# Two cross-attention layers in one program: the filler products of the first seven steps dealt out anew

## The chip, the cores and the metric

One Trainium2 chip; the program runs on one of its cores. The metric is the device time of one execution in microseconds (us), the median of several runs. The profile comes from one further look at the same program: the hardware profiler's record of one execution.

## What is computed

Two cross-attention layers follow each other, for 8 batches of 256 queries of width 320 (20 heads of 16) and 256 context tokens of width 512. The context's text tokens and its last few tokens (image tokens) have keys and values of their own.

```python
# layer 0: two softmaxes, 77 text tokens and 179 others
q = heads(x @ Wq.T); k = heads(text @ Wk.T); v = heads(text @ Wv.T)
k_ip = heads(ip @ Wk_ip.T); v_ip = heads(ip @ Wv_ip.T)
x = (attend(q, k, v) + attend(q, k_ip, v_ip)) @ Wo.T + bo + x
# layer 1: 252 text tokens, 4 image tokens
probs_t = softmax(q @ k_t.T * scale)
text_out = probs_t @ v_t
qsem = l2norm(probs_t @ text)              # 512 wide, per head
sem = qsem @ l2norm(ip).T
probs_ip = softmax(q @ k_ip.T * scale + 0.5 * sem) * mask
x = (text_out + probs_ip @ v_ip) @ W_out + b_out + x
```

The norm of `qsem` is taken without `qsem` itself: its square is a quadratic form of the probabilities with the gram matrix of the text tokens (252 x 252).

## The kernel before

The work is cut into steps. Each batch has 5 groups of 4 heads (`NQ` = 5), and step n does group n % 5 of batch n // 5 of layer 0, and, from step 6 on (`SHIFT` = 6), the group n - 6 of layer 1. The change concerns steps 0 to 6; step 7 is the last one with a list of its own. TensorE (PE), VectorE (DVE), ScalarE (ACT) and GpSimd (POOL) each run their instructions in the order in which the program issues them; no scheduler reorders them.

A step, function `both_layers`, issues in this order:

- the scores of the four heads (`scores`, L359), from `sc_qz`, queries with the other heads' rows masked out, and `k0`. The masked queries of step n + 1 (`masked_q`, L349) are made on GpSimd near the end of step n, behind everything that GpSimd was given before;
- the maxima on VectorE (L500), then the exponentials of heads 0 and 1 on ScalarE (L512);
- the fillers of place 0;
- the exponentials of heads 2 and 3;
- the transposes of heads 0 and 1 (L397), each copied to `et` (L404) by VectorE;
- the transposes of the previous group's output, its scaling (L555) and its sum on GpSimd (`attn`, L565);
- the fillers of place 1;
- the transposes of heads 2 and 3, the copy of the last one by ScalarE;
- the fillers of place 2; then the masked queries for the next step; then (from step 6) layer 1's scores, exponentials and transposes with the places 3 to 6;
- the value products of layer 0 (`l0_values`, L530) and the copy `oT_sb` by ScalarE (L540).

A filler is a piece of other work that is put into such a place: a product on TensorE into one of two PSUM buffers (`mm_tile`) and its copy out, the eviction. Its instructions stand in every engine's queue at the place where the filler is issued. The lists of `fillers` are written out by hand. The fillers that the change moves:

- `l0_q(b, ms)`: queries of layer 0, thirds `ms` (L292), evicted by ScalarE (L299). The last third serves group 4.
- `l0_k(b, m)`: keys (L310); for m = 2 four evictions by ScalarE (L468, L472), else one (L462).
- `l0_v(b, i)`: values (L322), evicted by ScalarE (L485, L487). Values have two buffers, one for each of two batches.
- `l1_gram(b, c)`: gram matrix (L621). For c = 0 it is 126 x 252, evicted by ScalarE in three pieces (L630), for c = 1 126 x 126 in one; then GpSimd copies it to nine further places of the tile `gv` (L634). The first layer-1 values that read `gv` are in step 7.
- `ip_squares`, `ip_norm`: squares and norms of all image tokens, on VectorE and ScalarE (a square root, L250, which needs another table of functions than the exponential); `ip_T` transposes them (L259), `ip_k` and `ip_v` make layer 1's image keys (L272) and values.
- `l1_q`, `l1_k`: queries and keys of layer 1.

In step 5 the fillers of place 2 are a chain: `l0_attn_T`, `l0_out`, then `l1_xT` and `l1_q` give layer 1 its first queries. The inputs of the second batch are loaded from ScalarE's queue: `encT` at the start of step 1, `xT` at the start of step 2.

Of the kernel before, what the change touches and what calls it, by code (L numbers as in the profile page):

```python
# [50 lines left out]
def kernel(  # L51
# [40 lines left out]
    def mm_tile(name):  # L92
        return ps_mm.tile([P, 512], F32, tag="mm", name=name)

    def bc(ap, shape):
        return ap.to_broadcast(shape)
# [512 lines left out]
    def l1_gram(b, c):  # L609
        r = bat[b]  # L610
        encT_b = r["encT"]
        if c == 0:
            r["gv"] = [
                bp.tile([TC1, NPAIR, w + 2 * WV], F32, tag=f"gv{i}", name=f"gv{i}_{b}")
                for i, w in enumerate((3 * TC1, TC1))
            ]
        gv = r["gv"][c]
        ps = mm_tile(f"g{c}_{b}")
        n = TXT1 - c * TC1
        for k in range(NE):  # L620
            nc.tensor.matmul(  # L621
                ps[:TC1, :n],
                encT_b[:, k, c * TC1 : (c + 1) * TC1],
                encT_b[:, k, c * TC1 : TXT1],
                start=(k == 0),
                stop=(k == NE - 1),
            )
        blocks = ((TC1, 2.0), (0, 1.0), (TC1, 2.0)) if c == 0 else ((0, 1.0),)
        for i, (t0, f) in enumerate(blocks):
            nc.scalar.mul(  # L630
                gv[:, 0, WV + i * TC1 : WV + (i + 1) * TC1], ps[:TC1, t0 : t0 + TC1], f
            )
        n = len(blocks) * TC1
        nc.gpsimd.tensor_copy(  # L634
            gv[:, 1:, WV : WV + n],
            bc(gv[:, 0, WV : WV + n].unsqueeze(1), [TC1, NPAIR - 1, n]),
        )
# [362 lines left out]
    def fillers(n, place):  # L1000
        b, s = divmod(n, NQ)
        ahead, now, last, old = b + 1, b, b - 1, b - 2
        plan = {
            (0, 0): [(l0_v, now, 2)],
            (0, 1): [(l0_q, now, (2,))],
            (0, 2): [(l0_attn_T, last, 0), (l1_image, old)],
            (0, 3): [(l0_attn_T, last, 1), (l0_out, last, 0), (l0_out, last, 1)],
            (0, 4): [(l1_k, last, 0)],
            (0, 5): [(l1_xT, last)],
            (0, 6): [(l1_q, last, (0, 1))],  # L1010
            (1, 0): [(l0_k, now, 1)],
            (1, 1): [(l1_q, last, (2,))],
            (1, 4): [(l1_k, last, 1)],
            (1, 5): [(l1_ip, now), (l1_gram, now, 0)],
            (2, 0): [(l1_v, now, 0)],
            (2, 1): [(l1_gram, now, 1), (l1_den, old), (l1_norm, old)],
            (2, 2): [(l0_k, now, 2)],
            (2, 4): [(l0_v, ahead, 0), (l1_fused, old)],
            (2, 6): [(l1_fused_exp, old)],
            (3, 0): [(l1_v, now, 1)],  # L1020
            (3, 3): [(l1_probs, old)],
            (3, 4): [(l0_q, ahead, (0, 1))],
            (3, 5): [(l1_probs_T, old), (l1_text, old), (l0_v, ahead, 1)],
            (4, 0): [(l0_k, ahead, 0)],
            (4, 1): [(l1_attn, old)],
            (4, 2): [(l1_attn_T, old, 0)],
            (4, 3): [(l1_attn_T, old, 1)],
            (4, 4): [(l1_out, old, 0)],
            (4, 5): [(l1_out, old, 1)],
        }  # L1030
        if n <= NQ + 2:
            plan = (
                {
                    0: [(l0_v, 0, 0), (l0_v, 0, 1)],
                    1: [(l0_v, 0, 2)],
                },
                {
                    0: [(l0_k, 0, 1)],
                    1: [(l0_k, 0, 2)],
                    2: [(l0_q, 0, (2,))],  # L1040
                },
                {
                    0: [(l1_gram, 0, 0), (l0_v, 1, 0)],
                    1: [(l0_k, 1, 0), (ip_squares, 0)],
                    2: [(ip_norm, 0)],
                },
                {
                    0: [(l0_v, 1, 1), (l0_q, 1, (0, 1))],
                    1: [(ip_T, 0), (l0_v, 1, 2)],
                    2: [(ip_v, 0)],  # L1050
                },
                {
                    0: [(l1_ip, 0), (l1_v, 0, 0), (l1_v, 0, 1)],
                    1: [(ip_k, 0), (l1_gram, 0, 1)],
                    2: [(ip_k, 1)],
                },
                {
                    0: [(l0_k, 1, 1), (ip_k, 2), (l0_q, 1, (2,))],
                    1: [(l1_k, 0, 0)],
                    2: [(l0_attn_T, 0, 0), (l0_attn_T, 0, 1), (l0_out, 0, 0), (l0_out, 0, 1)],  # L1060
                    5: [(l1_xT, 0)],
                    6: [(l1_q, 0, (0, 1))],
                },
                {
                    0: [(l1_k, 0, 1)],
                    1: [(l1_q, 0, (2,))],
                    2: [(l0_k, 1, 2)],
                    4: [(l1_ip, 1), (l1_gram, 1, 0)],
                    5: [(l1_gram, 1, 1)],
                },  # L1070
                {
                    0: [(l1_v, 1, 0)],
                    4: [(l0_v, 2, 0)],
                },
            )[n]
            plan = {(s, at): f for at, f in plan.items()}
        if b >= 3 and b % 2:

            plan[1, 0], plan[1, 1] = plan[1, 0] + plan[1, 1], []
        if b >= 2 and b % 2 == 0 and ahead < B:  # L1080
            plan[3, 4] = [(l0_v, ahead, 1)]
            plan[3, 5] = [(l1_probs_T, old), (l1_text, old), (l0_q, ahead, (0,))]
            plan[4, 0] = [(l0_q, ahead, (1,)), (l0_k, ahead, 0)]
        if (b, s) == (1, 4):
            plan[4, 4] = [(l0_v, ahead, 2)]
        if (b, s) == (2, 0):
            plan[0, 0], plan[0, 1] = plan[0, 1], []
        if b == B - 1:

            plan[0, 6] = []  # L1090
            plan[1, 0] = [(l1_q, last, (0, 1))]
            plan[1, 1] = [(l1_q, last, (2,))]
            plan[1, 5] = [(l0_k, now, 1)]
            plan[2, 0] = [(l1_ip, now), (l1_gram, now, 0)]
            plan[3, 4] = [(l1_k, now, 0)]
            plan[4, 0] = [(l1_v, now, 0)]
        if b == B:
            plan[0, 4] = [(l1_k, last, 1)]
            plan[1, 4] = []
        for f, at, *args in plan.get((s, place), ()):  # L1100
            if 0 <= at < B:
                f(at, *args)
# [22 lines left out]
    def both_layers(n, u, v1):  # L1125
# [7 lines left out]
        if late:  # L1133
            l0_exp(u0, 1)
        fillers(n, 0)
        if not late:
            l0_exp(u0, 1)
# [3 lines left out]
        l0_transposed(u0, 1)  # L1141
        part(l0_attn, u)
        fillers(n, 1)
        part(l1_values, v1, 1, (0,))
        l0_transposed(u0, 2)
        part(l1_values, v1, 1, (1,))

        l0_transposed(u0, 3, nc.vector.tensor_copy if n % NQ == 2 and n > 2 * NQ else None)
        fillers(n, 2)
        part(l1_values, v1, 2)  # L1150
        qz[1] = queries(1, n)
# [125 lines left out]
```

## Time and profile before

| | |
|---|---|
| median of 3 runs | 883.96 us (883.80 to 883.97) |
| the profiled execution | 883.8 us, of it 882.1 us span |
| TensorE busy | 865.1 us, 98% of the span |
| VectorE, ScalarE, GpSimd busy | 614.0, 546.0, 208.8 us |
| granted TensorE clock | 1.00 in all windows of the first 64 us |
| starts of layer 0's scores, steps 0 to 7 | 11.03, 22.50, 33.66, 44.90, 59.70, 71.38, 91.52, 110.32 us |

PE is TensorE's products, PEld its weight loads, which run beside the products before them. In a timeline line stand the start and the length in us, the engine, the line of the source, the operation, the tile written and those read, the shapes and the number of merged instructions, and in brackets the idle time of that engine before it and what ended it. "issue" means that nothing that the profile shows was waited for.

### The profile page before, as it was taken

How to read it: one execution, taken by the hardware profiler on the slowest of the kernel's cores; microseconds unless marked ns; L12 is line 12 of the kernel's file. 1: busy time of each engine (PE TensorE's matmuls, PEld its weight loads, DVE VectorE, ACT ScalarE, POOL GpSimd, SP SyncE). 2: the span in 40 equal slices, each digit the busy share in tenths (PEclk: the TensorE clock that was granted, in tenths of full speed). 3: DMA queues.
4: the chain of work that ended last, by engine and by line, in shares of the span. 5: the costliest groups of instructions: out<-in, count | busy, mean ns of one | idle time of the engine just before them, and what ended most of it. 6: DMA issues, size and time to landing. Idle time of an engine off the chain costs nothing.

```text
span 882.1 us, 18743 instructions
## 1 busy us (share of the span) xinstructions
PE 865.1 (98%) x6178; PEld 696.4 (79%) x6178; DVE 614.0 (70%) x2071; ACT 546.0 (62%) x2386; POOL 208.8 (24%) x376
## 2 busy tenths in 40 slices
PE   9999899999999999999999999999999999999997
PEld 6767678788787887888878888888888787777776
DVE  2544477767777777776778678776777778775765
ACT  4765666656755586555765468654675558654844
POOL 2212311223221222122321322212232122312111
PEclk9999999999999999999999999999999999999999
DMA  9600100001000100011001010000100100000000
GB/s 278 173 6 6 52 2 1 2 16 43 15 2 20 34 25 2 10 27 42 16 1 21 16 43 1 3 20 16 43 1 1 22 16 1 1 21 1 1 20 16
DMA packets 24624, 22.96 MB, mean 26 GB/s; under 512 B 5936, under 2 KB 24496, under 8 KB 24528
## 3 DMA queue, kind: packets, MB, share of 16 engines
q1 hardware_dynamic: 23088, 20.27, 8.7%
q10 hardware_dynamic: 1440, 1.49, 0.5%
q8 instruction: 50, 0.82, 0.4%
q14 instruction: 46, 0.38, 0.1%
HBM read 18.31 MB, written 2.62 MB: 24 GB/s over the span
## 4 chain that ended last, share of the span: by engine, by line
PE 85%; ACT 3%; DVE 1%; issue 0%; POOL 0%; ACTq 0%; DVEq 0%
PE y L752 17%; PE sc L397 15%; PE sc L359 9%; PE y L755 9%; PE v L322 9%; PE k L310 7%; PE q L292 6%; PE p_o L335 5%; PE oT L530 4%; PE g L621 2%; ACT e L728 1%; ACT e L512 1%; PE p_aT_ps L328 1%; PE o L550 1%; PE ipo L866 1%; PE x1T_ps L328 1%
## 5 line engine op out<-in xcount | busy, mean ns | idle before, releaser
L512 ACT ACTIVATE e<-sc,nmx 128x77 f32<-128x77 f32 (+1 forms) x640 | 227.2, 411 | 58.1 <-DVE nmx L500 56.4
L728 ACT ACTIVATE e<-sc,nmx 128x252 f32<-128x252 f32 x320 | 147.4, 484 | 119.5 <-DVE aip L708 106.2
L752 PE MATMUL y<-gv,et 126*128 126x272 f32 x640 | 202.1, 397 | 1.2
L759 DVE CUSTOM_DVE_ANT_0 e<-y,e 128x252 f32<-128x252 f32 x320 | 134.0, 419 | 93.2 <-PE y L755 84.9
L397 PE MATMUL sc<-ident,e 128*126 128x128 f32 (+1 forms) x1280 | 183.2, 274 | 6.2 <-ACT e L512 3.7
L404 DVE COPY et<-sc 128x512 f32<-128x512 f32 (+1 forms) x228 | 153.9, 689 | 24.7 <-PE sc L397 15.5
L500 DVE TENSOR_REDUCE nmx<-sc 128x2 f32<-128x154 f32 x320 | 109.7, 415 | 85.4 <-PE sc L359 85.4
L397 PEld LDWEIGHTS sc<-ident,e 128*126 128x126 f32 (+1 forms) x1280 | 148.7, 140 | 17.6 <-ACT e L512 8.2
L512 ACT ACTIVATION_READ_ACCUMULATOR e<-sc,nmx 128x1 f32 x640 | 159.5, 250 | 0.0
L755 PEld LDWEIGHTS y<-gv,et 126*128 126x128 f32 x640 | 120.7, 189 | 25.9
L755 PE MATMUL y<-gv,et 126*128 126x146 f32 x640 | 131.4, 287 | 0.0
L713 DVE TENSOR_REDUCE nmx<-sc 128x2 f32<-128x504 f32 x160 | 106.7, 674 | 24.2 <-PE sc L359 24.2
L565 POOL TENSOR_TENSOR attn<-o_sb 128x64 f32<-128x64 f32 x80 | 24.4, 327 | 405.4 <-DVE o_sb L555 365.5
L752 PEld LDWEIGHTS y<-gv,et 126*128 126x128 f32 x640 | 104.8, 190 | 18.1 <-issue 3.0
L404 ACT COPY et<-sc 126x512 f32<-126x512 f32 (+1 forms) x92 | 52.9, 593 | 74.2 <-PE sc L397 74.1
L359 PE MATMUL sc<-k,sc_qz 32*128 32x256 f32 x1152 | 82.5, 400 | 1.0 <-POOL sc_qz L349 1.0
L349 POOL TENSOR_SCALAR sc_qz<-q,quad_m 128x256 f32<-128x256 f32 x80 | 73.2, 925 | 7.3 <-ACT q L299 6.7
L359 PEld LDWEIGHTS sc<-k,sc_qz 32*128 32x128 f32 x1152 | 52.0, 184 | 24.4 <-issue 14.8
L728 ACT ACTIVATION_READ_ACCUMULATOR e<-sc,nmx 128x1 f32 x320 | 69.8, 218 | 0.0
L322 PE MATMUL v<-wv,encT 128*126 128x324 f32 (+1 forms) x192 | 58.1, 447 | 0.0
L763 DVE COPY num<-y 128x20 f32<-128x20 f32 x320 | 55.8, 174 | 0.0
L335 PE MATMUL p_o<-wo,p_aT 128*128 128x320 f32 x180 | 53.0, 437 | 0.3 <-DVE p_aT L329 0.3
(151 smaller groups left out, 1047.1 us busy)
## 6 DMA issues: line engine op xcount, KB each, us to landing
encT<-in_encT_dram SPq DMA_DIRECT2D x7, 512.0 KB
x<-in_x_dram SPq DMA_DIRECT2D x8, 320.0 KB
out_dram<-osb SPq DMA_DIRECT2D x15, 160.0 KB
xT<-in_xT_dram SPq DMA_DIRECT2D x7, 256.0 KB
texts<-in_encT_dram SPq DMA_DIRECT2D x6, 154.0 KB
xT<-in_xT_dram SPq DMA_DIRECT2D x7, 128.0 KB
vip_rows<-vipA SPq DMA_DIRECT2D x32, 25.0 KB
wv<-in_WvT_dram SPq DMA_DIRECT2D x1, 640.0 KB
```

Source lines behind the costliest of these rows:

```text
L322: nc.tensor.matmul(ps, lhsT(k), w[:, k, :], start=(k == 0), stop=(k == NE - 1))
L335: nc.tensor.matmul(ps[:, :C], aT[:, m, :], w[:, m, :], start=(m == 0), stop=(m == NC - 1))
L359: nc.tensor.matmul(sc[j][:, half, :], qz[rows, half * P : (half + 1) * P], kT(j)[rows, :], start=True, stop=True,)
L397: nc.tensor.transpose(v[:, c, half, :], u["e"][x][:, i, half, t0 + c * tn : t0 + (c + 1) * tn], ident,)
L404: copy(u["et"][x][:tn, i].rearrange("p c n s -> p (c n s)"), ps)
L500: nc.vector.tensor_reduce(u["nmx"][x][:, j, :, a], u["sc"][2 * x + j][:, :, t0:t1], AX.X, ALU.max, negate=True,)
L512: nc.scalar.activation(u["e"][x][:, j, half, t0:t1], u["sc"][2 * x + j][:, half, t0:t1], AF.Exp, bias=u["nmx"][x][:, j, half, a : a + 1], ...
L713: nc.vector.tensor_reduce(u["nmx"][x][:, j, :], u["sc"][2 * x + j][:, :, t0 : t0 + TXT1], AX.X, ALU.max, negate=True,)
L728: nc.scalar.activation(u["e"][x][:, j, half, t0 : t0 + TXT1], u["sc"][2 * x + j][:, half, t0 : t0 + TXT1], AF.Exp, bias=u["nmx"][x][:, j, ...
L752: nc.tensor.matmul(y, et[:, 1 - odd, half, :], gv[0][:, g, full], start=True, stop=False)
L755: nc.tensor.matmul(y[:, into], et[:, odd, half, :], gv[1][:, g, part], start=False, stop=True)
L759: nc.vector.tensor_tensor_reduce(e, y[:, g0 : g0 + TXT1], e, op0=ALU.mult, op1=ALU.add, scale=1.0, scalar=0.0, accum_out=r["n2"][:, half, ...
```

## The change

The lists for steps 1 to 6 are written anew. Nothing is added or left out. On GpSimd the copy L634 of the small gram part moves from step 4 to step 1, behind that step's `attn` and ahead of the masked queries for step 2; that of the large part stays in step 2 but moves from ahead of `attn` to behind it, again ahead of the masked queries. On ScalarE the evictions move with their products; on VectorE the copies of `ip_T` and `ip_k`. SyncE's queue keeps its order. The first lines let the tile `gv` be made by whichever gram part is issued first.

```diff
--- before.py
+++ after.py
@@ -609,7 +609,7 @@
     def l1_gram(b, c):
         r = bat[b]
         encT_b = r["encT"]
-        if c == 0:
+        if "gv" not in r:
             r["gv"] = [
                 bp.tile([TC1, NPAIR, w + 2 * WV], F32, tag=f"gv{i}", name=f"gv{i}_{b}")
                 for i, w in enumerate((3 * TC1, TC1))
@@ -1035,36 +1035,35 @@
                     1: [(l0_v, 0, 2)],
                 },
                 {
-                    0: [(l0_k, 0, 1)],
+                    0: [(l0_k, 0, 1), (l0_q, 0, (2,))],
                     1: [(l0_k, 0, 2)],
-                    2: [(l0_q, 0, (2,))],
+                    2: [(l1_gram, 0, 1)],
                 },
                 {
-                    0: [(l1_gram, 0, 0), (l0_v, 1, 0)],
+                    0: [(l0_v, 1, 0), (l0_v, 1, 1)],
                     1: [(l0_k, 1, 0), (ip_squares, 0)],
-                    2: [(ip_norm, 0)],
+                    2: [(ip_norm, 0), (l1_gram, 0, 0)],
                 },
                 {
-                    0: [(l0_v, 1, 1), (l0_q, 1, (0, 1))],
-                    1: [(ip_T, 0), (l0_v, 1, 2)],
+                    0: [(l0_q, 1, (0, 1)), (ip_T, 0)],
+                    1: [(l0_v, 1, 2)],
                     2: [(ip_v, 0)],
                 },
                 {
                     0: [(l1_ip, 0), (l1_v, 0, 0), (l1_v, 0, 1)],
-                    1: [(ip_k, 0), (l1_gram, 0, 1)],
-                    2: [(ip_k, 1)],
+                    1: [(ip_k, 0), (ip_k, 1)],
+                    2: [(ip_k, 2)],
                 },
                 {
-                    0: [(l0_k, 1, 1), (ip_k, 2), (l0_q, 1, (2,))],
+                    0: [(l0_k, 1, 1), (l0_q, 1, (2,))],
                     1: [(l1_k, 0, 0)],
                     2: [(l0_attn_T, 0, 0), (l0_attn_T, 0, 1), (l0_out, 0, 0), (l0_out, 0, 1)],
                     5: [(l1_xT, 0)],
                     6: [(l1_q, 0, (0, 1))],
                 },
                 {
-                    0: [(l1_k, 0, 1)],
-                    1: [(l1_q, 0, (2,))],
-                    2: [(l0_k, 1, 2)],
+                    0: [(l1_k, 0, 1), (l1_q, 0, (2,))],
+                    1: [(l0_k, 1, 2)],
                     4: [(l1_ip, 1), (l1_gram, 1, 0)],
                     5: [(l1_gram, 1, 1)],
                 },
```

## The prediction

> **What bounds the kernel now.** I read the page first, then the timeline of the first 112 us one engine at a time: TensorE's weight loads, ScalarE, GpSimd, VectorE. The page's first part and its chain say that TensorE sets the time:
>
> ```profile
> PE 865.1 (98%) x6178; PEld 696.4 (79%) x6178; DVE 614.0 (70%) x2071; ACT 546.0 (62%) x2386; POOL 208.8 (24%) x376
> PE 85%; ACT 3%; DVE 1%; issue 0%; POOL 0%; ACTq 0%; DVEq 0%
> ```
>
> The change leaves the amount of work as it is, so it can only move TensorE's idle time in the seven steps that it deals out. A step begins with the weight loads of its first layer's scores, L359. In the weight loads' timeline these lie at 22.50, 33.66, 44.90, 59.70, 71.38 and 91.52 us for steps 1 to 6, and at 110.32 for step 7. Some of these lines, and the gaps that matter, from that timeline (start, length, operation, count, idle time before it and what ended it):
>
> ```profile
> 32.58 0.67 PEld L530 LDWEIGHTS oT<-et,v 128*32 128x32 f32 x16 [0.33 <-issue]
> 33.66 0.74 PEld L359 LDWEIGHTS sc<-k,sc_qz 32*128 32x128 f32 x16 [0.41 <-issue]
> 44.90 0.74 PEld L359 LDWEIGHTS sc<-k,sc_qz 32*128 32x128 f32 x16 [0.41 <-issue]
> ...
> 71.38 0.74 PEld L359 LDWEIGHTS sc<-k,sc_qz 32*128 32x128 f32 x16 [0.41 <-POOL sc_qz L349]
> ...
> 95.11 0.42 PEld L397 LDWEIGHTS sc<-ident,e 128*128 128x128 f32 x4 [0.95 <-ACT e L512]
> 96.51 0.42 PEld L397 LDWEIGHTS sc<-ident,e 128*128 128x128 f32 x4 [0.98 <-ACT e L512]
> ```
>
> Two things are to be seen. Between the value products (L530) and the next scores there is a gap of 0.41 us in every step, and nothing waits there: the masked queries, sc_qz, are ready. And what idle time there is comes from the exponentials on ScalarE. The masked queries come from GpSimd, whose timeline has this:
>
> ```profile
> 39.33 3.02 POOL L634 COPY gv<-gv 126x3402 f32<-126x3402 f32 x1 [8.46 <-ACT gv L630]
> 42.32 1.04 POOL L565 TENSOR_TENSOR attn<-o_sb 128x64 f32<-128x64 f32 x2
> 43.34 0.92 POOL L349 TENSOR_SCALAR sc_qz<-q,quad_m 128x256 f32<-128x256 f32 x1
> ...
> 69.15 1.13 POOL L634 COPY gv<-gv 126x1134 f32<-126x1134 f32 x1 [0.91 <-ACT gv L630]
> 70.26 0.93 POOL L349 TENSOR_SCALAR sc_qz<-q,quad_m 128x256 f32<-128x256 f32 x1
> ```
>
> L634 spreads the product of the image and text tokens (the gram tile) over nine more head pairs: 3.02 us for the large part, 1.13 us for the small one. It stands ahead of sc_qz in GpSimd's order. In step 2 sc_qz ends at 44.26, 0.64 us before the scores begin, though the gram product was the first filler of its step. In step 4 it ends at 71.19, 0.19 us before the scores. So there is next to no slack behind a gram filler. Last, ScalarE, at the end of step 2 and in step 5:
>
> ```profile
> 43.28 0.59 ACT L404 COPY et<-sc 128x512 f32<-128x512 f32 x1 [0.54 <-PE sc L397]
> 43.88 1.28 ACT L250 ACT_TABLE_LOAD   x1
> 45.18 0.20 ACT L250 ACTIVATE ip_rn<-ip_rn 32x1 f32<-32x1 f32 x1
> ...
> 77.58 0.39 ACT L299 ACTIVATE q<-q 128x256 f32<-128x256 f32 x1 [1.00 <-PE q L292]
> ```
>
> **The change, step by step.** The profiled run took 883.8 us with a span of 882.1 (1.7 us lie around it); the median of the runs is 883.96. Both gram fillers move to the last place of their step, just ahead of the masked queries on GpSimd. The new order there is attn, L634, sc_qz in step 1 and again in step 2. This adds a wait: sc_qz stands behind L634, which waits for ScalarE's eviction L630, which stands behind the last copy et (L404). The next scores on TensorE, and all that follows them there, wait for sc_qz.
>
> Step 1 (from 22.50). The last third of the queries moves to the first place: 1.17 us of loads on TensorE, hidden because the second transposes wait for the exponentials until 27.50 anyway. Its eviction now stands between the two halves of the exponentials, 0.26 us (27.29 to 27.55 is the pitch of such a copy). Exponentials end 30.52 + 0.26 = 30.78; four copies of k take 1.52 (30.52 to 32.04), so 32.30; et 0.60, so 32.90; the gram eviction 0.35 (its like stands at 68.74), so 33.25; 0.06 to GpSimd; L634 1.12, so 34.43; sc_qz 0.93, so 35.36; 0.1 to 0.19 to the scores. They start at 35.5 instead of 33.66: **+1.8**. TensorE itself is done with the values at about 33.2. Bounds +1.6 to +2.0, by the two gaps and by 0.2 us for the copies.
>
> Step 2. Its first place now has two value products of the second batch (2.00 us each: 45.97 to 47.97), for the gram (1.60) and one of them (2.09). The second's eviction waits for its product at +5.5 us from the step's start, so the second half of the exponentials starts at +5.97 instead of +5.84, 0.13 later. The copy et then ends at +10.34 (43.87 is +10.21 now). Behind it come the table load and the square root of ip_norm, up to +11.76 (45.29 less 43.87 is 1.42). Only then the three gram evictions, 0.64: +12.40. GpSimd: 0.06, L634 3.02, sc_qz 0.93, 0.1: scores at +16.5. TensorE has finished gram and values at about +12.0 and idles for 4 us or so. The step lasts 16.5 instead of 11.24: **+5.3**, bounds +5.0 to +5.6. In this sum the 2.00 us of the product that came from step 3 are contained.
>
> Step 3. VectorE's scaling of ip_n (1.22 us at 45.60) now falls into that idle time. The first maximum begins at 1.16 us from the step's start instead of 2.01 (46.91): 0.85 sooner, and the exponentials' table load (1.28) with it: exponentials from +3.22. First place: queries 2.65, ip_T 0.61 and a 0.17 gap, done at +4.5; the first transposes' e is ready at +4.65. ScalarE has one eviction less between the halves (0.41 us), so the second half ends at +9.35, and the last transposes at +9.75. ip_v with its gap takes 1.81 (56.40 to 58.21), the values to the next scores 1.49 (58.21 to 59.70): 13.0 instead of 14.80: **-1.8**, bounds -1.4 to -2.2 by the 0.41 us eviction either way.
>
> Step 4. The gram (0.88 us of loads) leaves the middle place and a product of image keys (0.89) takes it; another moves up to the last place. ScalarE has one eviction of 0.35 less, but et waited 0.64 us for the transposes there, and these for the last exponential. **0**, bounds -0.2 to +0.1.
>
> Step 5. The image keys' last product leaves the first place, 1.01 us of loads with a wait of 0.39 behind it. The queries' product follows k at once, at 74.55, and ends at 76.05. Its eviction now waits for it until 77.58, after the k copy's pitch ends at 76.43; that idle time goes, and the second half of the exponentials starts at 76.69 instead of 77.86: **-1.15**. What is late next are the transposes that wait for it (80.81), so all of it counts; the chain behind them (attn_T, out, x1T, queries) moves as a whole. Bounds -1.4 (1.01 + 0.39) and -0.4 (only TensorE's own wait).
>
> Step 6. The second layer's queries join the first place; 1.17 us fill the wait of 0.95 ahead of the first transposes. k of the second batch moves from the end to the middle, ahead of the last transposes, into the wait of 0.86. Against it: an eviction of 0.26 between the halves, and four k copies (1.49) ahead of et. Exponentials end 99.47 + 0.26 = 99.73, k copies 101.22, et 101.82. The layer's second scores can finish loading at 102.6 instead of 103.5; the exponentials behind them start up to 1.3 sooner (104.45 to 103.15). **-1.1**, bounds -0.5 to -1.3.
>
> Sum: 1.8 + 5.3 - 1.8 + 0 - 1.15 - 1.1 = **+3.05 us**. From step 7 on the order is the same and TensorE is busy for 19.6 to 20.0 of each 20 us (120 to 200 us), so the shift is kept to the end. 883.8 + 3.05 = 886.85 for a run like the profiled one; by the median **887.0**. All low ends together give 1.6 + 5.0 - 2.2 - 0.2 - 1.4 - 1.3 = +1.5, all high ones 2.0 + 5.6 - 1.4 + 0.1 - 0.4 - 0.5 = +5.4: 885.5 to 889.4.
>
> [...] The longest idle time of TensorE's loads within these steps is now 0.98 us, and the granted clock is 1.00 throughout; but the first eight products after the start took 3.78 us for 256 columns each, against 2.75 us for twelve of that width at 48.23. If a pace of 0.47 us for 0.23 came back behind the 4 us gap, scores and queries of step 3 (3.7 us of loads) would take twice as long, and with some 1.4 to 2 us of it not hidden by the exponentials, the time would be about 889.0. [...]
>
> **The rivals.**
> The gap is followed by a slow stretch, as above: 889.0. For it, the slow start; against, no slow products anywhere later.
> Steps 5 and 6 give nothing back, because other waits take the place (POOL's attn for attn_T, et behind four k copies): 887.0 + 2.25 = 889.3. Against it, attn is ready at 80.32 before attn_T at 81.20 and moves with it.
> The opposite side: sc_qz doesn't bind, because L634 is done early enough. It decides if L634 ends 0.93 us ahead of the values. Then steps 1 and 2 cost only TensorE's own work: step 1 about -0.1, step 2 +12.4 instead of 11.24, so +1.2, and the rest stays: -0.1 + 1.2 - 1.8 - 1.15 - 1.1 = -2.95, that is **881.0**. Against it, the order on GpSimd and the 0.19 us that were left in step 4 with the gram one place earlier.
> That the waits come half as long, a total near +1, is the last: it needs step 2's eviction to pass the table load.
>
> **How the numbers follow.** Forecast 0.70, slow stretch 0.11, nothing back 0.09, no binding 0.05, half 0.05. A difference of 0.2% (1.77 us, up from 885.73) is about what can be told from none. Faster 0.05, same 0.07, slower 0.88. Range 885.6 to 889.3: it holds nearly all between the forecast's bounds, and both slow rivals' middles.
>
> **What would show it.** Right: in the changed trace the scores of steps 2 and 3 begin at about 35.5 and 52.0 us, with idle loads of some 2 and 4 us ended by POOL's sc_qz; steps 4 to 6 at 65.0, 76.7, 95.7, step 7 at 113.4; ScalarE's q eviction of step 5 with no wait of 1.00. Wrong: scores of step 3 before 48, or a q wait that returns in step 5, or a granted clock below 1.00 after 50 us.

## The result and the profile after

The changed kernel takes 888.61 us (median of 6 runs, 887.61 to 889.21) against 883.97 before: 4.64 us longer, ratio 1.0052 with a 95% interval of 1.0042 to 1.0063. The forecast was 887.0, slower; the time lies in the range, 1.6 us above the forecast and 0.4 us below the rival with the slow stretch.

The profiled execution took 887.61 us with a span of 885.9. Its weight loads on TensorE, at the starts of steps 2, 3, 4 and 7 (columns as before: start, length, operation, count, idle time and what ended it):

```profile
35.30 0.74 PEld L359 LDWEIGHTS sc<-k,sc_qz 32*128 32x128 f32 x16 [1.71 <-POOL sc_qz L349]
...
46.65 0.59 PEld L530 LDWEIGHTS oT<-et,v 128*32 128x32 f32 x16 [0.33 <-issue]
51.74 1.00 PEld L359 LDWEIGHTS sc<-k,sc_qz 32*128 32x128 f32 x16 [4.50 <-POOL sc_qz L349]
53.40 3.52 PEld L292 LDWEIGHTS q<-xT,wq 128*128 128x128 f32 x12 [0.65 <-issue]
...
65.58 0.74 PEld L359 LDWEIGHTS sc<-k,sc_qz 32*128 32x128 f32 x16 [0.41 <-issue]
...
114.19 0.74 PEld L359 LDWEIGHTS sc<-k,sc_qz 32*128 32x128 f32 x16 [0.41 <-issue]
```

Two gaps stand there that the kernel before did not have: the scores of step 2 and of step 3 follow 1.71 and 4.50 us after the load before them, where the usual gap is 0.41, and what ended them is sc_qz on GpSimd. Counted from product to product, TensorE was without one for 1.22 and 4.02 us. GpSimd's and ScalarE's timelines show what sc_qz waited for:

```profile
33.21 1.13 POOL L634 COPY gv<-gv 126x1134 f32<-126x1134 f32 x1 [2.88 <-ACT gv L630]
34.32 0.92 POOL L349 TENSOR_SCALAR sc_qz<-q,quad_m 128x256 f32<-128x256 f32 x1
...
47.74 3.04 POOL L634 COPY gv<-gv 126x3402 f32<-126x3402 f32 x1 [3.60 <-ACT gv L630]
50.77 0.92 POOL L349 TENSOR_SCALAR sc_qz<-q,quad_m 128x256 f32<-128x256 f32 x1
```

```profile
45.72 1.28 ACT L250 ACT_TABLE_LOAD   x1
47.01 0.20 ACT L250 ACTIVATE ip_rn<-ip_rn 32x1 f32<-32x1 f32 x1
47.12 0.56 ACT L630 ACTIVATE gv<-g 126x126 f32<-126x126 f32 x3
```

The chain of step 2 stands there as it was worked out: table load, square root, three evictions, L634, sc_qz, scores. GpSimd itself idled for 3.60 us ahead of L634, so it is the place in its order that costs, not its load. (The prediction calls L634's tile a product of image and text tokens; the kernel makes it from the text tokens alone, as said under "What is computed". No time hangs on that.)

Step 3 shows something more. After the gap the 16 loads of the scores take 1.00 us instead of 0.74, the 12 of the queries 3.52 instead of 2.62, which they took in the kernel before:

```profile
47.97 2.62 PEld L292 LDWEIGHTS q<-xT,wq 128*128 128x128 f32 x12
```

The stretches of 2 us around it (busy time of PE, PEld, DVE, ACT and POOL with the number of instructions, then granted TensorE clock, DMA share and GB/s):

```profile
48.00:50.00 2.00, 0.00 (x0) 0.00 (x0) 0.07 (x1) 0.22 (x1) 2.00 (x1) 1.00 0.00 0
50.00:52.00 2.00, 0.25 (x4) 0.26 (x8) 0.00 (x0) 0.00 (x0) 2.00 (x4) 1.00 0.00 0
52.00:54.00 2.00, 2.00 (x18) 1.20 (x15) 0.53 (x2) 0.00 (x0) 1.96 (x4) 0.54 0.00 0
54.00:56.00 2.00, 2.00 (x7) 1.66 (x6) 2.00 (x7) 1.67 (x4) 0.00 (x0) 0.60 0.00 0
56.00:58.00 2.00, 2.00 (x16) 1.52 (x15) 0.24 (x2) 2.00 (x14) 0.00 (x0) 1.00 0.00 0
```

The granted clock falls to 0.54 and 0.60 in the 4 us behind the gap, and is back at 1.00 from 56 us on. The only other place where the trace reads below 0.99 is its last microsecond (0.56), when TensorE has nothing left to do.

The lengths of the steps, from scores to scores of layer 0, in us (all from the weight loads' timelines; the last two columns are experiments below):

| step | before | forecast | changed kernel | queries ahead (e1_both) | and the table (f4_table) |
|---|---|---|---|---|---|
| 1 | 11.16 | 13.0 | 12.55 | 11.23 | 11.25 |
| 2 | 11.24 | 16.5 | 16.44 | 12.35 | 12.36 |
| 3 | 14.80 | 13.0 | 13.84 | 13.27 | 12.00 |
| 4 | 11.68 | 11.7 | 11.67 | 11.66 | 11.67 |
| 5 | 20.14 | 19.0 | 19.04 | 19.02 | 19.04 |
| 6 | 18.80 | 17.7 | 17.90 | 17.86 | 17.88 |
| sum | 87.82 | 90.9 | 91.44 | 85.39 | 84.20 |

Steps 1 to 6 are 3.62 us longer. Step 1 itself began 0.25 us later (22.75 for 22.50), although nothing ahead of it was changed; in the experiments that start lies between 22.52 and 23.08. Together that is 3.87, and the span grew by 3.8: in this execution nothing is lost or won from step 7 on.

### The profile page after: what moved, and what is told of

Its sections match the earlier page's. It is cut to its first block, busy times and chain, and to the rows that moved or that the text cites. A ratio compares the mean times of both kernels' runs of the same rounds, so it can differ in the third digit from the quotient of the medians.

```text
span 885.9 us, 18744 instructions
## 1 busy us (share of the span) xinstructions
PE 865.7 (98%) x6178; PEld 696.7 (79%) x6178; DVE 612.0 (69%) x2071; ACT 545.4 (62%) x2386; POOL 208.5 (24%) x376
## 3 DMA queue, kind: packets, MB, share of 16 engines
HBM read 18.31 MB, written 2.62 MB: 24 GB/s over the span
## 4 chain that ended last, share of the span: by engine, by line
PE 91%; ACT 4%; issue 2%; DVE 1%; POOL 1%; DMA 1%; SPq 0%; ACTq 0%; DVEq 0%; POOLq 0%
PE y L752 17%; PE sc L397 15%; PE v L322 10%; PE sc L359 10%; PE y L755 9%; PE k L310 7%; PE q L292 6%; PE p_o L335 6%; PE oT L530 4%; ACT e L512 2%; PE g L621 2%; ACT e L728 1%; PE p_aT_ps L328 1%; PE o L550 1%; PE ipo L866 1%
```

## The experiments

Each is timed in five rounds beside the kernel before, whose median was 883.61 us in the first four and 883.78 in the last four.

**e1_both: the order on GpSimd alone.** In `both_layers`, for n = 1 and n = 2:

```diff
+        first = n in (1, 2)
+        if first:
+            qz[0] = queries(0, n + 1)
         fillers(n, 2)
         part(l1_values, v1, 2)
         qz[1] = queries(1, n)
-        qz[0] = queries(0, n + 1)
+        if not first:
+            qz[0] = queries(0, n + 1)
```

> The masked queries of steps 2 and 3 are issued ahead of the last place's fillers of steps 1 and 2, so on GpSimd sc_qz stands ahead of L634; nothing else changes. Theory (sc_qz behind L634 holds the scores of both steps, and the 4 us of idle TensorE halve its clock for a while): the scores of step 2 begin 1.3 us sooner from the start of step 1 (values' loads end at 33.59, the usual 0.41 behind them is 34.00 instead of 35.30), those of step 3 4.1 us sooner (46.65 + 0.59 + 0.41 = 47.65 instead of 51.74), and the slow stretch goes: 0.9 us in the profiled run, up to 2 in the slower runs. Time 881.2 us, between 880.6 and 882.3, below the kernel before. Rival 1 (the cost is the moved work itself: two value products in step 2, an eviction more among the exponentials): 888 or so, the same waits at another place. Rival 2 (the queries' place is right, but the table load and ip_norm hold step 3 in its place): steps 2 and 3 together as long as in the kernel before (26.0 us), time about 883.5.

Measured: 881.3 us, ratio to the kernel before 0.9974 (0.9965 to 0.9984). Every filler lies where the changed kernel has it; only sc_qz passed L634. The weight loads at the starts of steps 2 and 3:

```profile
33.75 0.74 PEld L359 LDWEIGHTS sc<-k,sc_qz 32*128 32x128 f32 x16 [0.41 <-issue]
46.10 0.74 PEld L359 LDWEIGHTS sc<-k,sc_qz 32*128 32x128 f32 x16 [0.41 <-issue]
```

Both gaps are the usual 0.41. Steps 1 and 2 are shorter by 1.32 and 4.09 us, as expected. The moved work as such does not cost what was lost (rival 1). Rival 2 put the kernel at 883.5, which it beat; but its length for steps 2 and 3 together, 26.0 us, is near the 25.62 measured, and f4_table below shows that a table load does hold step 3. The gain over the kernel before lies elsewhere, as f3_nolate shows.

**e2_step1 and e3_step2: one of the two waits at a time.** The same edit with `n in (1,)` and `n in (2,)`.

> Only the masked queries of step 2 are issued ahead of the gram filler of step 1; in step 2 the order stays as in the changed kernel. Theory: step 1 lasts 11.25 us instead of 12.55, the gap of 4 us in step 2 and the slow clock behind it stay: 888.6 - 1.3 = 887.3, and its runs spread over more than 1 us as those of the changed kernel do. If moved work were the cost: no change, 888.6.

> Only the masked queries of step 3 are issued ahead of the large gram filler of step 2; step 1 stays as in the changed kernel. Theory: step 2 lasts 12.35 us instead of 16.44, the longest idle time of TensorE is the 1.7 us in step 1, the granted clock stays at 1.00 and step 3 lasts 13.0 instead of 13.84: 882.6 us, and the runs agree within 0.3 us again. Without a slow clock as a cause of its own: 887.6 - 4.1 = 883.5 with the changed kernel's spread.

Measured: 886.37 us (ratio 1.0032, 1.0019 to 1.0044) for the first, 882.58 (0.9989, 0.9980 to 0.9998) for the second. In e2_step1 step 1 lasts 11.23 us and the gap of 4.50 stays, with a clock of 0.50 in 52 to 54 us. In e3_step2 the gap of 1.71 stays, step 2 lasts 12.36, step 3 13.26, and the clock stays at 1.00. So the wait in step 2 is the larger part and brings the slow clock; the wait in step 1, with 1.71 us, does not. Two misses: e2_step1 came out 0.9 us below what was expected, and its runs spread over 0.67 us only. Of the 0.9 us, 0.36 are the kernel before, which was that much faster beside these runs than beside the first ones; the cause of the rest stays open. In its trace step 3 lasts 13.52 us, 0.32 less than in the changed kernel, but the control below has 13.53 with the gap where the changed kernel has it, so the earlier gap is not the reason. For e3_step2 step 3 was expected at 13.0 us, 0.26 too short, and its runs spread over 0.52 us instead of 0.3.

**e4_warm: TensorE kept busy in the gap.**

```diff
         l0_values(u0)
+        if n == 2:
+            ps = mm_tile("warm")
+            for _ in range(8):
+                nc.tensor.matmul(ps[:, :P], ident, ident, start=True, stop=True)
         return u0, u1
```

> The changed kernel with eight further products of the identity with itself (128 x 128, into a PSUM tile that nobody reads) behind the values of step 2; the masked queries stay behind L634. They add about 2 us of TensorE work inside the gap, which then is about 2.2 us of idle time. Theory of the slow clock: scores of step 3 begin at the same 51.7, the granted clock is 1.00 in 52 to 56 us, step 3 lasts 13.0 us instead of 13.84, the median falls from 888.6 to about 886.8 and the runs agree within 0.4 us. Rival (the longer step 3 and the spread come from something else, for instance from transfers): nothing changes, 888.6 with a spread of over 1 us.

Measured: 886.67 us (886.55 to 887.04; ratio 1.0037, 1.0024 to 1.0049). TensorE's products around the gap:

```profile
47.51 2.05 PE L1171 MATMUL warm<-ident 128*128 128x128 f32 x16
51.60 1.15 PE L359 MATMUL sc<-k,sc_qz 32*128 32x256 f32 x16 [2.04 <-POOL sc_qz L349]
52.67 2.86 PE L292 MATMUL q<-xT,wq 128*128 128x256 f32 x12
```

Each of the eight calls shows as two products. The scores wait for sc_qz as before, but the products behind the gap run at their usual pace, the granted clock reads 1.00 and step 3 lasts 13.26 us. In the changed kernel the same products took 1.72 and 3.92 us:

```profile
51.75 1.72 PE L359 MATMUL sc<-k,sc_qz 32*128 32x256 f32 x16 [4.02 <-POOL sc_qz L349]
53.40 3.92 PE L292 MATMUL q<-xT,wq 128*128 128x256 f32 x12
```

Against its own kernel before this is +3.06 us: the two waits and the moved work without a slow stretch in the trace. Additional work made the changed kernel faster. Of its five runs three had a mean clock of 0.999 (the kernel before has 0.999 or 1.0), and two (886.97 and 887.04) had 0.998; whether these lost clock in the shorter gap no trace shows.

**f1_again and f2_warm2: the control, and only two products in the gap.** `f1_again` is the changed kernel; `f2_warm2` has `range(2)` in the edit above.

> The changed kernel once more, as the control on the same chip for the two with further products in the gap. Theory: 4.0 us of TensorE without a product in step 2, the granted clock near a half for about 3.4 us behind it, times between 887.2 and 889.0 with a spread of over 1 us, about 2 above the kernel with eight further products (886.67).

> The changed kernel with two further products of the identity (instead of eight) behind the values of step 2: about 0.5 us of work, so that 3.5 us of the gap stay without a product (eight left 2.0). [...]

Measured: 888.94 us (887.11 to 889.0) for the control, 5.16 above its kernel before; 887.23 (886.81 to 888.2) with two products, 3.45 above. The first products of step 3 in the control, then in f2_warm2:

```profile
51.91 1.42 PE L359 MATMUL sc<-k,sc_qz 32*128 32x256 f32 x16 [4.02 <-POOL sc_qz L349]
53.27 4.22 PE L292 MATMUL q<-xT,wq 128*128 128x256 f32 x12
```

```profile
51.86 1.15 PE L359 MATMUL sc<-k,sc_qz 32*128 32x256 f32 x16 [3.38 <-POOL sc_qz L349]
```

In the control's profile the clock reads 1.00 from 51 to 52 us, 0.83 in the next, 0.50 from 53 to 56 and 0.96 from 56 to 57: 1.7 us of clock lost, as in the first profile, but step 3 lasts 13.53 us there instead of 13.84. In the profile of f2_warm2 TensorE had 3.38 us without a product ahead of the scores and the clock stayed at 1.00. The mean clock of each timed run tells more: of the five runs it was 0.999 once (886.81), 0.998 three times (887.12 to 887.23) and 0.996 once (888.2). In the control it was 0.998 once (887.11, the profiled run) and 0.996 in the four others (888.47 to 889.0). A mean of 0.998 over 886 us is a loss of 1.3 to 2.2 us of clock, as the mean is rounded, one of 0.996 a loss of 3.1 to 4.0; the two slow windows of the first profile hold 2 x 0.46 + 2 x 0.40 = 1.72. A mean also counts the 3.5 us behind the last product, where a slow clock costs no time: there the trace of before lost 0.96 us of clock and that of the changed kernel 0.44. Even so, a run at 0.996 lost at least 0.4 us more than the slow stretch of the profiles and the longer of these two ends together. That was so in five of the first six runs and four of the five of the control, and it goes with medians 1.0 and 1.8 us above the profiled runs, though one run at 0.996 (887.79) lies only 0.2 above. Where this further clock was lost no trace shows, and it stays open.

**f3_nolate: steps 5 and 6 put back.** On e1_both:

```diff
-                    2: [(ip_k, 2)],
...
-                    0: [(l0_k, 1, 1), (l0_q, 1, (2,))],
+                    0: [(l0_k, 1, 1), (ip_k, 2), (l0_q, 1, (2,))],
...
-                    0: [(l1_k, 0, 1), (l1_q, 0, (2,))],
-                    1: [(l0_k, 1, 2)],
+                    0: [(l1_k, 0, 1)],
+                    1: [(l1_q, 0, (2,))],
+                    2: [(l0_k, 1, 2)],
```

> The kernel with both masked queries ahead (881.3) in which steps 5 and 6 have their fillers as in the kernel before: the last image keys between k and q in step 5, q and k of step 6 at places 1 and 2. Theory (steps 5 and 6 give 1.1 and 0.9 us): step 5 lasts 20.1 us instead of 19.0 and step 6 18.8 instead of 17.9; step 4 loses its last filler and is 0.3 shorter. Time 883.0, between 882.6 and 883.5. If instead the gain of that kernel comes from steps 1 to 3 alone: 881.3 or below.

Measured: 883.65 us, ratio 0.9998 (0.9989 to 1.0007), just above the expected range. Step 5 lasts 20.13 us, step 6 18.78: the gains of 1.1 and 0.9 us come from these two places. Without them the kernel is as fast as the one before, so they are most of what e1_both gained; steps 1 to 3 together last 36.85 us there against 37.20 before. The miss: step 4 lasts 11.64, not 0.3 less; without its last filler its value products wait 0.65 us for the copy et. ScalarE's eviction of the queries in step 5 has its wait back, which it had lost in the changed kernel (no idle time ahead of it there, at 82.30 us):

```profile
77.24 0.38 ACT L299 ACTIVATE q<-q 128x256 f32<-128x256 f32 x1 [1.01 <-PE q L292]
```

**f4_table: the exponential's table loaded ahead of need.** On e1_both, behind the gram filler of step 2:

```diff
+    def exp_table(_):
+        table(AF.Exp)
...
-                    2: [(ip_norm, 0), (l1_gram, 0, 0)],
+                    2: [(ip_norm, 0), (l1_gram, 0, 0), (exp_table, 0)],
```

> The kernel with both masked queries ahead (881.3), and one more tiny exponential on ScalarE behind the gram evictions of step 2, so that the table of the exponential is loaded (1.28 us) while the maxima of step 3 are not there yet. Theory (step 3 is bound by its exponentials, which the table load pushes back): the first exponential of step 3 starts right behind the first maxima, step 3 lasts about 12.0 us instead of 13.27, time 880.1. If TensorE's own products bound step 3: no change, 881.3. If the load pushes back the copy oT_sb and with it the transposes of step 2's output: 881.3 to 881.8.

Measured: 879.97 us (879.9 to 880.12), ratio 0.9956 (0.9943 to 0.997), the fastest of all. ScalarE's timeline at the end of step 2 (this kernel's lines stand 3 further down, so L633 is the L630 of above):

```profile
45.66 0.56 ACT L633 ACTIVATE gv<-g 126x126 f32<-126x126 f32 x3
46.24 1.28 ACT L789 ACT_TABLE_LOAD   x1
47.53 0.20 ACT L789 ACTIVATE one<-msk 128x1 f32<-128x1 f32 x1
47.64 0.35 ACT L543 COPY oT_sb<-oT 128x256 f32<-128x256 f32 x1
48.23 0.33 ACT L515 ACTIVATE e<-sc,nmx 128x77 f32<-128x77 f32 x1 [0.23 <-DVE nmx L503]
```

In the kernel before, the load of 1.28 us stood behind the maxima, after an idle time of 2.05 us that ended with nmx:

```profile
47.68 1.28 ACT L512 ACT_TABLE_LOAD   x1 [2.05 <-DVE nmx L500]
```

In e1_both ScalarE was busy for 0.50 us from 46 to 48 us and for 1.87 us, with four instructions, from 48 to 50 us; by an estimate from these figures the load stood behind them there too. Now the first exponential follows them after 0.23 us idle, and step 3 lasts 12.00 us instead of e1_both's 13.27.

## Why the prediction was right, and where it was not

The direction and the two waits came as foreseen, and with them most of the signs named for being right: the scores of steps 2 and 3 at 35.30 and 51.74 us behind sc_qz, step 5's eviction without a wait. But one of the signs named for being wrong came too, a granted clock below 1.00 after 50 us, and the measured time is nearer to the rival that has it (889.0) than to the forecast (887.0).

**The wait in step 2**: forecast +5.3, measured +5.20. Shown by e3_step2 and e1_both. This is the step that decided the sign.

**The wait in step 1**: forecast +1.8, measured +1.39, below its bounds of +1.6 to +2.0. The mechanism is right (e2_step1), the size was 0.4 off. The sum put 0.26 us of eviction on top of the end of the exponentials, taken as 30.52 us in the trace of before. But 30.52 was the start of the k copies, and these came 0.04 us behind the end of their own product, 29.06 + 1.42 = 30.48, where the pitch of the exponentials would have let them start near 30.3. In the changed kernel the exponentials began 0.27 later and the copies stand at +8.07 us from the step's start instead of +8.02: that wait took up 0.2 of it. The other 0.2 lie behind: from the start of et to that of L634 it took 0.83 us (32.38 to 33.21) instead of the 1.01 of the sum, and the scores followed sc_qz by 0.06 us. The start of a row is not the end of the work ahead, even where no idle time is shown: for each row one has to ask what else it waited for.

**Step 3**: forecast -1.8, measured -0.96, outside its bounds of -1.4 to -2.2. At full clock it is 13.26 us (e4_warm), so the estimate of the reordered step was 0.26 short and the slow clock took 0.58 us in the profiled run (0.27 in the control's).

**Step 4**: 0, as forecast. **Step 5**: -1.15 forecast, -1.10 measured. **Step 6**: -1.1 forecast, -0.90 measured, within its bounds. f3_nolate shows both places.

**The slow stretch**: this is the term that the forecast left out of its sum. It was a rival with a chance of 0.11 and a time of 889.0; it came true in every timed run of the changed kernel (mean clock at most 0.998 in all eleven, with f1_again). Without it the sum of +3.05 stands at +3.06 in e4_warm, so close by luck: the terms that were off, -0.4 in step 1 and -0.1 in step 2 against +0.26 in step 3 and +0.2 in step 6, cancel. With it the medians were +4.64 and +5.16, so it is worth 1.6 to 2.1 us, about the rival's 2. The rival's reckoning does not fit the traces, though: of one stretch at half pace 1.4 to 2 us were to be added, and in the traced runs step 3 grew by 0.58, 0.27 and 0.26 us (e2_step1 the last). In the first two that is by how much the score products alone took longer, 1.72 and 1.42 us for 1.15; the longer queries behind them, 3.92 and 4.22 us for 2.86, added nothing to the step. What the medians show beyond that goes with the further clock lost in the untraced runs, whose place no trace shows; so the rival's price came out partly by luck. The forecast had the gap, its 4 us and the row that shows the slow pace of the first products (there the granted clock reads 1.00), and gave it too little weight.

After how long without a product the clock falls, the runs do not settle. With 4.02 us all eleven timed runs had lost clock. With 3.38 us one run of five had 0.996 and three 0.998, but 0.998 came twice with 2.04 us as well. And at the end of the trace of before the last product ends at 878.58, while the microsecond from 880.10 reads 0.54 and the next 0.50: by these figures the clock fell about 1.6 us behind the last product; in the changed kernel, where it ends at 882.40 and the last microsecond reads 0.56, about 2.6 us. For the rival the prediction named only the slow start; this end of the same trace speaks for it too.

**The rival on the other side** can be checked once the order is turned: without binding sc_qz it has -2.95 us, 881.0; e1_both measured 881.3, which is -2.31 against its own kernel before. That the wait did bind was argued from the order on GpSimd and the 0.19 us left in step 4.

## What to carry to other kernels

A filler that was put where TensorE has room also takes a place in every other queue: before moving one, follow its last instruction on each engine and see what stands behind it there. Here 3 us of a copy that nobody needed for five steps held up the queries that everybody waited for, and issuing those first turned 4.6 us lost into 2.3 us won. The gap of 4.02 us in TensorE cost more here than its length: the slow stretch behind it was worth 1.6 to 2.1 us by the medians, and a forecast with such a gap has to weigh it.

## What the runs showed of the hardware that was not expected

The granted clock fell not in the gap of 4.02 us but, by an estimate from 1 us stretches, 0.4 to 0.75 us after products had begun again: the first stretch below 1.00 read 0.59, 0.83 and 0.74 in the changed kernel, its control and e2_step1 (there from 0.87 over 2 us). It was back at 1.00 from 56 us on in the changed kernel and from 57 us on in its control; the 1.7 us of clock that each of these three traces lost make about 3.4 us at a half. With 2.04 and with 3.38 us without a product the profiles show no drop, though the mean of 0.996 in one run with 3.38 us suggests that it can fall there too, and at the end of the trace of before it fell after some 1.6 us. The wait in step 1 (1.22 us without a product) had no such effect: all eleven runs of e3_step2 had means of 0.999 or 1.0. And in the kernel before a table load on ScalarE ran only after the wait of the exponential that needed it (1.28 us at 47.68, behind 2.05 us of idle time): a tiny exponential put ahead took 1.27 us off step 3, which lasts 12.00 us in f4_table for 13.27 in e1_both.
